# A sparse attention layer on one core: the first sort moved into the stream of its lists, feed-forward endings cut into steps, a sixth gather buffer and an earlier verdict

## The chip, the core and the metric

The kernel runs on one core of a Trainium2 chip. The core's engines work side by side, each through its own queue in order: TensorE (PE in the profile, PEld for its weight loads), VectorE (DVE), ScalarE (ACT), GpSimd (POOL) and SyncE (SP). SP, ACT and POOL also issue DMA transfers. The metric is the device time of one execution in microseconds (us), smaller is better.

## The reference, cut to what matters

One graph attention layer with a feed-forward block: N = 4096 nodes, D = 512, 8 heads of 64, float32. `adj` has a one for about 0.4% of the pairs and on the diagonal.

```
hs, ht = layer_norm(x), layer_norm(h_target)
q, k, v = ht @ Wq / 8, hs @ Wk, hs @ Wv            # per head
probs   = softmax(where(adj != 0, q k^T, -1e30))
ht      = layer_norm(ht + (probs @ v) @ Wo)
ff      = gelu(ht @ W1) @ W2                       # W1 512 x 2048, W2 2048 x 512
out     = layernorm(x + ht + ff)
```

## The kernel before

Since a row of `adj` has some 17 neighbours, the kernel never forms the 4096 x 4096 logits. It makes **lists** of neighbours, sorts the target nodes by degree, and then, tile by tile of 128 sorted targets, gathers one row of K and V (1024 floats) for each neighbour slot.

**Projections** (`project`). 16 groups of 256 source rows give K and V (`source`, L769), written to `kvd` in HBM (L773). 16 groups of target rows give q and a residual (`target`, L780), written to `tqd` (L791). Each group is normalised (`norm`: L628 on DVE, the power L622 on POOL, L623 on DVE, L741 on ACT), transposed (`turn`, L755) and multiplied. The targets form two parts: part 0 has 20 tiles (10 groups), part 1 has 12 tiles (6 groups, `qb`).

**Lists** (`edges`). For each of 32 tiles, four loads of `adj` on SP's queue (L637), a Sign on ACT (L640), and on DVE products and maxima (L642, L644), then 5 rounds of maximum and replace (L659, L661) that leave up to 40 neighbours in the record `R`.

**Sort** (`sort(part)`). A counting sort by degree: a one-hot `oh` (L687), four small matmuls (L697, L704) with scans between, ranks (L710), and one indirect store per tile on POOL (L713, 20 of them in part 0) that scatters the records to HBM. Its PSUM tile `t` is the one that `turn` uses too.

**Attention** (`attention`). Per tile, `prefetch` loads the sorted record (L824, SP), `front` gathers the targets' rows (`tq`, L812), and the neighbours are taken in stages of up to 3 slots. For a stage `issue` gathers 3 tiles of K and V (L812 on POOL, one instruction for each slot, into a `kv` buffer of 3 x 1024 floats); DVE multiplies by q (L944) and reduces (L948); ACT takes the exponential (L952); one stage later `values` multiplies V (L921), and PE sums by transposing into `cps` (L925), which frees the buffer. There are 5 `kv` buffers and `AHEAD = 3`. `finish` ends a tile: the softmax's sum, `Wo` (L882), `h` (L885), the norm (L621 to L623, L893) and its transposes (L901).

**Feed-forward** (`feed`). 17 groups of one or two tiles. `hidden` is W1 (L989) and gelu (L992), `output` is W2 (L998). The sums `po` begin with the transposes L1015, written after the second `hidden`. When a group ends, DVE adds (L1026), takes statistics, POOL the power (L622), DVE scales (L1030), and POOL stores the rows (L1032). `x` for the group is gathered half way (`xt`, L812).

**The order.** `_weave` merges generators by a clock of estimated costs, which each `yield` advances; nothing of it exists at run time. A compiler's scheduler takes the written order as priority, and may put a ready instruction further ahead in its engine's queue. Three weaves follow each other: (1) the projections of all sources and of part 0, beside the lists of part 0; (2) the rest of the projections, beside `begin` (sort of part 0, first records and gathers), from 55 the first 26 half stages of the attention, and from 60 two more tiles of lists; (3) the attention, the feed-forward, and the remaining 10 lists with the second sort. The weights `w1`, `w2` are loaded in quarters: the first between weaves 1 and 2 (when the sources' pool `src` is closed), three between 2 and 3 (when `mid` is closed). At the very end a verdict (did all sums, degrees and counts fit?) goes to `flag`, and `general_path` would run if it said no; with these inputs it does not run.

Of the kernel before, what the change touches and what calls it, by code (L numbers as in the profile page):

```python
# [17 lines left out]
P = 128  # L18
# [357 lines left out]
MAXE = 40  # L376
# [54 lines left out]
def adj_resnorm_kernel(  # L431
# [47 lines left out]
    SEGS = [(s * WQ // SQ, (s + 1) * WQ // SQ) for s in range(SQ)]  # L479
# [35 lines left out]
    with tc.tile_pool(name="keep", bufs=1) as keep:  # L515
# [14 lines left out]
        with ExitStack() as late:  # L530
            lp = late.enter_context(tc.tile_pool(name="lists", bufs=1))
            kp = late.enter_context(tc.tile_pool(name="kv", bufs=5))
# [19 lines left out]
            R = lp.tile([P, NT, RW], I32, name="R")  # L552
# [3 lines left out]
            iota_i = lp.tile([P, P], I32, name="iota_i")  # L556

            segoff = lp.tile([P, 2, NQ, SQ], F32, name="segoff")
            for b in range(2):
                for s, (w0, _) in enumerate(SEGS):  # L560
                    nc.gpsimd.iota(iota_i[:, :NQ], pattern=[[QW, NQ]], base=2 * w0 + b,
                                   channel_multiplier=0)
                    nc.vector.tensor_copy(segoff[:, b, :, s], iota_i[:, :NQ])

            nc.gpsimd.iota(iota_i, pattern=[[2, P]], base=1, channel_multiplier=0)
            lio = lp.tile([P, WQ], U16, name="lio")
            for w0, w1 in SEGS:
                nc.vector.tensor_copy(lio[:, w0:w1], iota_i[:, :w1 - w0])
            nc.gpsimd.iota(iota_i, pattern=[[1, P]], base=0, channel_multiplier=0)
            bins = lp.tile([P, NB], BF16, name="bins")  # L570
            nc.vector.tensor_copy(bins, iota_i[:, :NB])

            lower = lp.tile([P, P], BF16, name="lower")
            nc.gpsimd.memset(lower, -1.0)
            nc.gpsimd.affine_select(out=lower, in_=lower, compare_op=ALU.is_ge, fill=0.0, base=0,
                                    pattern=[[-1, P]], channel_multiplier=1)
            nc.gpsimd.memset(R, 0)
            nc.gpsimd.iota(R[:, :, MAXE + 1], pattern=[[P, NT]], base=0, channel_multiplier=1)
            for i0, n in PARTS:
                nc.gpsimd.iota(R[:, i0:i0 + n, MAXE + 2], pattern=[[P, n]], base=0,  # L580
                               channel_multiplier=1)
            one_c = lp.tile([P, 1], F32, name="one_c")
            nc.vector.memset(one_c, 1.0)
# [32 lines left out]
            def rstd_of(pool, mv, n, name):  # L616

                ve = pool.tile([P, n], F32, name=name + "_ve")
                rs = pool.tile([P, n], F32, name=name + "_rs")
                nm = pool.tile([P, n], F32, name=name + "_nm")  # L620
                nc.vector.tensor_scalar_add(ve, mv[:, :, 1], EPS)  # L621
                nc.gpsimd.tensor_tensor(rs, ve, mhalf[:, :n], ALU.pow)  # L622
                nc.vector.scalar_tensor_tensor(nm, mv[:, :, 0], -1.0, rs, op0=ALU.mult, op1=ALU.mult)  # L623
                return rs, nm
# [7 lines left out]
            def edges(i):  # L632

                cand = lp.tile([P, SEG, 8], U16, name="cand", bufs=2)
# [22 lines left out]
                for r in range(MAXE // 8):  # L657
                    top = R[:, i, r * 8:(r + 1) * 8]
# [4 lines left out]
                nc.vector.tensor_scalar(has, R[:, i, :MAXE], 0.0, 0.0, op0=ALU.is_gt,  # L663
# [7 lines left out]
            def sort(part):  # L671
# [3 lines left out]
                pool = lp  # L675
                nc.vector.tensor_reduce(deg[:, me], dpart[:, me, :], AX.X, ALU.add)
                nc.vector.tensor_copy(R[:, me, MAXE], deg[:, me])
# [7 lines left out]
                oh = pool.tile([P, NB * NA], BF16, name="oh")  # L685
# [26 lines left out]
                for i in range(n):  # L712
                    ins = nc.gpsimd.indirect_dma_start(  # L713
                        out=recs_d[part][:, :],
                        out_offset=bass.IndirectOffsetOnAxis(ap=ranki[:, i:i + 1], axis=0),
                        in_=R[:, i0 + i, :], in_offset=None)
# [135 lines left out]
            def finish(i, p, cps, group, hs, mv):  # L852
# [56 lines left out]
            def attention():  # L909
# [59 lines left out]
                while tails:  # L969
                    advance()  # L970
                    yield 3.0


            def feed(g):
# [49 lines left out]
                mv = sp.tile([P, 2, 2], F32, name="mv3")  # L1024
                for j in range(nt):
                    nc.vector.tensor_add(xs[j], po[j], xs[j])  # L1026
                    stats(sp, xs[j], mv[:, j, :], "n3")
                rs, _ = rstd_of(sp, mv[:, :nt, :], nt, "n3")
                for j, i in enumerate(group):
                    nc.vector.tensor_scalar(xs[j], xs[j], mv[:, j, 0:1], rs[:, j:j + 1],  # L1030
                                            op0=ALU.subtract, op1=ALU.mult)
                    ins = nc.gpsimd.indirect_dma_start(  # L1032
                        out=out[:, :], out_offset=bass.IndirectOffsetOnAxis(
                            ap=recs[i][:, MAXE + 1:MAXE + 2], axis=0),
                        in_=xs[j], in_offset=None)

                    tc.declare_no_dep(ins.ins, group="out", reason="other rows")
                    tc.add_to_no_dep_group("out", ins.ins)
# [6 lines left out]
            AHEAD = 3  # L1045
# [19 lines left out]
            wp1 = late.enter_context(tc.tile_pool(name="s2wa", bufs=1))  # L1065
            w1 = [wp1.tile([P, KC, D], F32, name="w1_0")]
            w2 = [wp1.tile([P, KC, D], F32, name="w2_0")]

            def load_quarter(q):
# [3 lines left out]
            load_quarter(0)  # L1073
            att = attention()
            early = 2 * sum(1 for i, _, _ in SG if i < 3)

            def begin():
# [10 lines left out]
            for q in range(1, 4):  # L1088
                w1.append(wp2.tile([P, KC, D], F32, name=f"w1_{q}"))
                w2.append(wp2.tile([P, KC, D], F32, name=f"w2_{q}"))  # L1090
                load_quarter(q)
# [8 lines left out]


        with tc.tile_pool(name="s3", bufs=1) as sp, \
                tc.tile_pool(name="s3ps", bufs=1, space=PSUM) as ps:
            sf = sums.rearrange("p t h -> p (t h)")
            ok = sp.tile([P, NT * H], F32, name="ok")
            nc.vector.tensor_scalar(ok, sf, SUM_LO, None, op0=ALU.is_gt)
            nc.vector.scalar_tensor_tensor(ok, sf, SUM_HI, ok, op0=ALU.is_lt, op1=ALU.mult)
            nc.vector.tensor_reduce(bad[:, 3:4], ok, AX.X, ALU.min)
            nc.vector.tensor_scalar(bad[:, 3:4], bad[:, 3:4], 1.0, None, op0=ALU.not_equal)
            over = sp.tile([P, NT], F32, name="over")  # L1110
            for i in range(NT):
                nc.vector.tensor_scalar(over[:, i:i + 1], degs[:, i:i + 1], float(TILES[i][1]), None,
                                        op0=ALU.is_gt)
            nc.vector.tensor_reduce(bad[:, 4:5], over, AX.X, ALU.max)
            nc.vector.tensor_scalar(over, degs, 1.0, None, op0=ALU.is_lt)
            nc.vector.tensor_reduce(bad[:, 5:6], over, AX.X, ALU.max)
            b1 = sp.tile([P, 1], BF16, name="b1")
            nc.vector.tensor_reduce(b1, bad, AX.X, ALU.max)
            pb = ps.tile([1, 1], F32, name="pb")
            nc.tensor.matmul(pb, b1, ones_bf[:, 0:1], start=True, stop=True)  # L1120
            nc.vector.tensor_scalar(flag, pb, 0.5, None, op0=ALU.is_gt)
# [35 lines left out]
```

## Time and profile before

| | us |
|---|---|
| median of 3 runs | 2008.25 (2004.03 to 2009.7) |
| the profiled execution | 2004.54 |
| its span, first to last instruction | 2002.8 |

| | busy us | share of the span |
|---|---|---|
| PE | 1751.0 | 87% |
| DVE | 1599.0 | 80% |
| POOL | 959.0 | 48% |
| ACT | 774.0 | 39% |

The profile's page gives busy shares, the same in 40 slices of the span, DMA queues, the chain of waits that ended last, and the costliest groups of instructions by line. The trace behind it answers for any stretch of time: busy time by engine with the clock that TensorE was granted, waits by who waited for whom, and the timeline. The lines that matter are shown in the prediction.

### The profile page before, as it was taken

The numbers are of one execution on the slowest core, as the hardware profiler recorded it, in microseconds if no ns is written. First come the engines' busy times: TensorE is split into PE (matmuls) and PEld (weight loads), VectorE is DVE, ScalarE is ACT, GpSimd is POOL, SyncE is SP. The second block draws the span as 40 slices with busy tenths as digits, with TensorE's granted clock in tenths as the row PEclk, the third lists the DMA queues.
The fourth block names the chain that finished last, engine by engine and source line by source line (L and its number), as shares of the span: only waits on it lengthen the run. The fifth ranks groups of instructions, "written<-read, shape, count | busy, mean of one in ns | idle before, by whom it ended". The sixth has DMA issues, their size and how long they took to land. (4 is left out here: it accounts for less than half of the span.)

```text
span 2002.8 us, 21520 instructions
## 1 busy us (share of the span) xinstructions
PE 1751.0 (87%) x7282; PEld 1133.6 (57%) x7282; DVE 1599.0 (80%) x2865; ACT 774.0 (39%) x1236; POOL 959.0 (48%) x879
## 2 busy tenths in 40 slices
PE   6989899762789999999798998989988889899996
PEld 3444444331556666666566666666665656567664
DVE  5989893356989999999788898988988878778601
ACT  5666564221245454452232333333323233333310
POOL 1023333164544546555666657657656554456301
PEclk9999999985979999998899999999999999999998
DMA  8778774479678888785578778868877766577300
GB/s 287 261 272 269 266 263 148 171 274 360 218 267 283 278 287 279 262 296 195 188 265 288 252 273 269 273 228 283 276 273 254 269 231 220 202 252 247 132 1 23
DMA packets 145391, 482.33 MB, mean 241 GB/s; under 512 B 20292, under 2 KB 20856, under 8 KB 145272
## 3 DMA queue, kind: packets, MB, share of 16 engines
q0 software_dynamic: 100032, 359.45, 52.2%
q1 hardware_dynamic: 39536, 102.53, 15.6%
q10 hardware_dynamic: 5704, 18.89, 2.4%
q8 instruction: 60, 0.98, 0.2%
q14 instruction: 59, 0.48, 0.1%
HBM read 438.07 MB, written 42.73 MB: 240 GB/s over the span
## 5 line engine op out<-in xcount | busy, mean ns | idle before, releaser
L812 POOL DMA_INDIRECT kv<-kvd,rec x600 | 687.6, 1146 | 464.6 <-PE cps L925 250.1
L989 PE MATMUL pf<-h2T,w 128*128 128x256 f32 (+1 forms) x2176 | 485.9, 374 | 3.6 <-ACT h2T L905 3.6
L998 PE MATMUL po<-w,gt 128*128 128x512 f32 x1024 | 471.1, 597 | 3.2 <-ACT gt L992 3.2
L944 DVE TENSOR_TENSOR kv<-kv,tq 128x1536 f32<-128x1536 f32 (+2 forms) x210 | 351.2, 1674 | 130.5 <-DMA kv<-kvd,rec 118.1
L989 PEld LDWEIGHTS pf<-h2T,w 128*128 128x128 f32 x2176 | 394.0, 195 | 77.2 <-issue 28.3
L925 PE MATMUL cps<-ident,kv 128*128 128x128 f32 x2400 | 320.4, 285 | 94.6 <-DVE kv L921 88.7
L925 PEld LDWEIGHTS cps<-ident,kv 128*128 128x128 f32 x2400 | 286.4, 147 | 169.3 <-DVE kv L921 127.3
L921 DVE TENSOR_TENSOR kv<-kv,p 128x1536 f32<-128x1536 f32 (+2 forms) x210 | 349.3, 1666 | 33.2 <-ACT p L952 33.0
L948 DVE TENSOR_REDUCE lg<-kv 128x24 f32<-128x1536 f32 (+2 forms) x210 | 349.3, 1666 | 0.5
L998 PEld LDWEIGHTS po<-w,gt 128*128 128x128 f32 x1024 | 186.5, 192 | 177.6 <-issue 171.6
L640 ACT ACTIVATE sg<-a 128x1024 uint8<-128x1024 int32 x128 | 135.0, 1055 | 146.5 <-DMA a<-in_adj_dram 90.4
L622 POOL TENSOR_TENSOR n_rs<-n_ve,mhalf 128x2 f32<-128x2 f32 (+1 forms) x66 | 55.0, 833 | 262.2 <-DVE n_ve L621 230.1
L952 ACT ACT_TABLE_LOAD x86 | 110.3, 1283 | 169.4 <-DVE lg L948 139.8
L952 ACT ACTIVATE p<-lg 128x24 f32<-128x24 f32 (+2 forms) x178 | 34.3, 193 | 320.3 <-DVE lg L948 161.4
L992 ACT ACTIVATE gt<-pf 128x512 f32<-128x512 f32 x128 | 76.5, 598 | 210.7 <-PE pf L989 190.2
L992 ACT ACT_TABLE_LOAD x111 | 142.4, 1283 | 2.0
L882 PE MATMUL t<-wo,rb 128*128 128x512 f32 x256 | 122.4, 623 | 20.3 <-DVE rb L878 20.3
L780 PE MATMUL pq<-wq,hT 128*128 128x512 f32 x256 | 125.2, 635 | 14.1 <-ACT row L771 7.5
L644 DVE MAX8 cand<-wd 128x8 uint16<-128x102 uint16 (+1 forms) x640 | 130.8, 251 | 0.8
L769 PE MATMUL pq<-wv,hT 128*128 128x512 f32 x256 | 116.1, 596 | 7.6 <-DVE row L783 6.8
L769 PE MATMUL pq<-wk,hT 128*128 128x512 f32 x256 | 116.0, 596 | 6.0 <-ACT row L771 3.7
L780 PEld LDWEIGHTS pq<-wq,hT 128*128 128x128 f32 x256 | 51.0, 206 | 78.8 <-issue 60.1
(122 smaller groups left out, 1452.0 us busy)
## 6 DMA issues: line engine op xcount, KB each, us to landing
a<-in_adj_dram SPq DMA_DIRECT2D x128, 512.0 KB
kvd<-row ACTq DMA_DIRECT2D x32, 512.0 KB
tq<-row POOLq DMA_DIRECT2D x20, 512.0 KB
kv<-kvd,rec POOLq DMA_INDIRECT x600
xin<-in_L_gnn_h_target_dram SPq DMA_DIRECT2D x16, 512.0 KB
w<-in_L_gnn_W_dram SPq DMA_DIRECT2D x8, 1024.0 KB
xin<-in_x_dram SPq DMA_DIRECT2D x15, 512.0 KB
tq<-row SPq DMA_DIRECT2D x12, 512.0 KB
```

What stands on the lines that cost most here:

```text
L640: nc.scalar.activation(sg, a, AF.Sign, accum_out=dpart[:, i, h:h + 1])
L769: nc.tensor.matmul(pkv, hT[:, kc, j * P:(j + 1) * P], w[:, kc, :], start=kc == 0, stop=kc == KC - 1)
L780: nc.tensor.matmul(pq, hT[:, kc, j * P:(j + 1) * P], wq[:, kc, :], start=kc == 0, stop=kc == KC - 1)
L812: nc.gpsimd.indirect_dma_start(out=dst, out_offset=None, in_=table[:, :], in_offset=bass.IndirectOffsetOnAxis(ap=idx, axis=0))
L921: nc.vector.tensor_tensor(v4, v4, p[:, j0:j0 + n, :].unsqueeze(3) .to_broadcast([P, n, H, HD]), ALU.mult)
L925: nc.tensor.matmul(cps[:, c, :], kv[:, j, D + c * P:D + (c + 1) * P], ident, is_transpose=True, start=j0 + j == 0 and c == 0, stop=j0 + j ...
L944: nc.vector.tensor_tensor(kv[:, :n, :D], kv[:, :n, :D], tq[:, :D].unsqueeze(1).to_broadcast([P, n, D]), ALU.mult)
L948: nc.vector.tensor_reduce(lg[:, :n, :], kv[:, :n, :D].rearrange("p j (h d) -> p j h d", h=H), AX.X, ALU.add)
L952: nc.scalar.activation(p[:, j0:j0 + n, :], lg[:, :n, :], AF.Exp)
L989: nc.tensor.matmul(pf[:, k, :], w1[(f0 + k) // KC][:, kc, (f0 + k) % KC * P:((f0 + k) % KC + 1) * P], h2T[:, kc, :w], start=kc == 0, stop= ...
L992: nc.scalar.activation(gt, pf, AF.Gelu_apprx_tanh)
L998: nc.tensor.matmul(po[j], gt[:, k, j * P:(j + 1) * P], w2[(f0 + k) // KC][:, (f0 + k) % KC, :], start=False, stop=f0 + k == FC - 1, skip_g ...
```

## The change

- **Part 0's sort** and first records join the stream of its lists in the first weave (`prepare`); `begin` then starts the attention 12 units after the records are there, in the same weave. `fill` makes three tiles of part 1's lists as soon as part 0's are done; 9 are left for the last weave. The four streams now run in one weave up to the closing of `mid`.
- **Constants** of the lists are written after the first projection's norm, with fewer and larger instructions. `R` and `oh` of part 0 move to the projections' pool, which gives room for
- **six `kv` buffers** instead of five, with `AHEAD = 4`.
- **Feed-forward ends** become a generator of four steps (`end`), one of which is taken after each of the next group's first four `hidden` (`wind_up`); `finish` too gets its power in a step of its own.
- **The verdict** is written at the end of the attention instead of the end of the kernel.

```diff
-    SEGS = [(s * WQ // SQ, (s + 1) * WQ // SQ) for s in range(SQ)]
+    WS = -(-WQ // SQ)
+    SEGS = [(s * WS, min(s * WS + WS, WQ)) for s in range(SQ)]
...
-            kp = late.enter_context(tc.tile_pool(name="kv", bufs=5))
+            kp = late.enter_context(tc.tile_pool(name="kv", bufs=6))
...
-            R = lp.tile([P, NT, RW], I32, name="R")
+            Rs = [pool.tile([P, n, RW], I32, name=f"R{i}")
+                  for i, (pool, (_, n)) in enumerate(zip((wp, lp), PARTS))]
...
+            def list_constants():
+                io = lp.tile([P, QW], I32, name="a", bufs=2)
+                nc.gpsimd.iota(io[:, :SQ * WS], pattern=[[0, SQ], [2, WS]], base=1,
+                               channel_multiplier=0)
...
-                oh = pool.tile([P, NB * NA], BF16, name="oh")
+                if part:
+                    oh = sp.tile([P, MAXE, H], F32, name="pm", bufs=1)
+                    oh = oh.rearrange("p j h -> p (j h)").bitcast(BF16)
+                else:
+                    oh = wp.tile([P, NB * n], BF16, name="oh")
...
-                rs, nm = rstd_of(sp, mv[:, :len(hs), :], len(hs), "n2")
+                nh = len(hs)
+                ve = shifted(sp, mv[:, :nh, :], nh, "n2")
                 yield
+                rs = power(sp, mv[:, :nh, :], nh, "n2", ve)
+                yield
+                nm = negmean(sp, mv[:, :nh, :], rs, nh, "n2")
...
                 while tails:
                     advance()
                     yield 3.0
-
+                verdict()
...
+            def end(group, xs, po):
+
+                nt = len(group)
+                mv = sp.tile([P, 2, 2], F32, name="mv3")
+                for j in range(nt):
+                    nc.vector.tensor_add(xs[j], po[j], xs[j])
+                    stats(sp, xs[j], mv[:, j, :], "n3")
+                ve = shifted(sp, mv[:, :nt, :], nt, "n3")
+                yield
+                rs = power(sp, mv[:, :nt, :], nt, "n3", ve)
+                yield
+                for j in range(nt):
+                    nc.vector.tensor_scalar(xs[j], xs[j], mv[:, j, 0:1], rs[:, j:j + 1],
+                                            op0=ALU.subtract, op1=ALU.mult)
+                yield
+                for j, i in enumerate(group):
+                    ins = nc.gpsimd.indirect_dma_start(
...
+                def wind_up():
+                    for e in list(ends):
+                        if next(e, StopIteration) is StopIteration:
+                            ends.remove(e)
+
                 last = hidden(0)
+                wind_up()
                 yield cost
                 for f0 in range(fb, FC, fb):
                     now = hidden(f0)
+                    wind_up()
                     yield cost
...
-            AHEAD = 3
+            AHEAD = 4
...
-            _weave((_take(proj, both * G), 0), (_take(ed, NA * steps), 0))
-            src.close()
...
             next(proj)
+            list_constants()
...
+            def projections():
+                yield from _take(proj, both * G)
+                src.close()
+                load_quarter(late.enter_context(tc.tile_pool(name="s2wa", bufs=1)), 0)
+                yield from proj
+
+            def prepare():
+
+                yield from _take(ed, NA * steps)
+                ready.append("lists")
                 yield from sort(0)
+                while not w1:
+                    yield None
                 for i in range(2):
                     prefetch(i)
                 next(att)
+                ready.append("rows")
+
+            def fill():
+
+                while not ready:
+                    yield None
+                for cost in _take(ed, 3 * steps):
+                    yield 2.0 * cost
+
+            def begin():
+                while len(ready) < 2:
+                    yield None
+                yield 12.0
+                yield from _take(att, early)
...
-            _weave((proj, 0), (begin(), 0), (_take(att, early), 55), (_take(ed, 2 * steps), 60))
+            _weave((projections(), 0), (prepare(), 0), (fill(), 0), (begin(), 0))
             mid.close()
```

More of the change, by code (lines that the diff above doesn't have):

```diff
@@ L632, in edges @@
             def edges(i):
+                part = 1 if i >= NA else 0
+                rec = Rs[part][:, i - PARTS[part][0], :]
                 cand = lp.tile([P, SEG, 8], U16, name="cand", bufs=2)
@@ L662, in edges @@
                 has = lp.tile([P, MAXE], F32, name="ehas")
[L663 removed]
+                nc.vector.tensor_scalar(has, rec[:, :MAXE], 0.0, 0.0, op0=ALU.is_gt,
                                         op1=ALU.add, accum_out=cnt[:, i:i + 1])
@@ L971, in attention, with verdict @@
                     yield 3.0
+                verdict()
+            def verdict():
+                sf = sums.rearrange("p t h -> p (t h)")
+                both = sp.tile([P, MAXE, H], F32, name="pm", bufs=1).rearrange("p j h -> p (j h)")
+                ok, over = both[:, :NT * H], both[:, NT * H:NT * H + NT]
+                nc.vector.tensor_scalar(ok, sf, SUM_LO, None, op0=ALU.is_gt)
+                nc.vector.scalar_tensor_tensor(ok, sf, SUM_HI, ok, op0=ALU.is_lt, op1=ALU.mult)
+                nc.vector.tensor_reduce(bad[:, 3:4], ok, AX.X, ALU.min)
+                nc.vector.tensor_scalar(bad[:, 3:4], bad[:, 3:4], 1.0, None, op0=ALU.not_equal)
+                for i in range(NT):
+                    nc.vector.tensor_scalar(over[:, i:i + 1], degs[:, i:i + 1], float(TILES[i][1]),
+                                            None, op0=ALU.is_gt)
+                nc.vector.tensor_reduce(bad[:, 4:5], over, AX.X, ALU.max)
+                nc.vector.tensor_scalar(over, degs, 1.0, None, op0=ALU.is_lt)
+                nc.vector.tensor_reduce(bad[:, 5:6], over, AX.X, ALU.max)
+                b1 = sp.tile([P, 1], BF16, name="b1", bufs=1)
+                nc.vector.tensor_reduce(b1, bad, AX.X, ALU.max)
+                pb = ps.tile([1, 1], F32, name="t")
+                nc.tensor.matmul(pb, b1, ones_bf[:, 0:1], start=True, stop=True)
+                nc.vector.tensor_scalar(flag, pb, 0.5, None, op0=ALU.is_gt)
@@ new lines, in adj_resnorm_kernel @@
+            ends = []
+            def end(group, xs, po):
[14 more added lines that the diff above has]
+                    ins = nc.gpsimd.indirect_dma_start(
+                        out=out[:, :], out_offset=bass.IndirectOffsetOnAxis(
+                            ap=recs[i][:, MAXE + 1:MAXE + 2], axis=0),
+                        in_=xs[j], in_offset=None)
+                    tc.declare_no_dep(ins.ins, group="out", reason="other rows")
+                    tc.add_to_no_dep_group("out", ins.ins)
@@ L1023, in feed @@
                 yield cost
[L1024 to L1038, printed above, removed]
+                ends.append(end(group, xs, po))
+                if g + 1 == len(GROUPS):
+                    for _ in ends.pop():
+                        pass
             def chain(gens):
@@ L1081, in begin @@
                 next(att)
-            _weave((proj, 0), (begin(), 0), (_take(att, early), 55), (_take(ed, 2 * steps), 60))
+                ready.append("rows")
[9 more added lines that the diff above has]
+                yield from _take(att, early)
+            ready = []
+            att = attention()
+            early = 2 * sum(1 for i, _, _ in SG if i < 3)
+            _weave((projections(), 0), (prepare(), 0), (fill(), 0), (begin(), 0))
             mid.close()
@@ L1099, in adj_resnorm_kernel @@
                    (other_lists(), t0))
[L1102 to L1121, printed above, removed]
     left = nc.values_load(flag[0:1, 0:1], min_val=0, max_val=1)
```

76 lines of the change are left out of this document (38 added, 38 removed).

## The prediction, made before the result was known

> **What bounds the kernel now.** I began with the page's 40 slices, 50 us each (digits are tenths busy; PEclk is the clock that TensorE was granted).
>
> ```profile
> span 2002.8 us, 21520 instructions
> PE   6989899762789999999798998989988889899996
> DVE  5989893356989999999788898988988878778601
> PEclk9999999985979999998899999999999999999998
> ```
>
> Three regimes show. Up to slice 6 PE is nearly full (projections). In slices 7 to 11 both PE and DVE fall, the clock with them. From slice 12 (600 us) PE stands at 8 or 9, DVE beside it. So there is no single bound: where PE is full, only PE's work counts; where both have holes, something else ends last. Hence the busy table by stretch: from:to, length, then PE, PEld, DVE, ACT and POOL with instructions, PE's clock, DMA share, GB/s.
>
> ```profile
> 310.00:367.00 57.00, 56.48 (x162) 26.95 (x160) 13.86 (x37) 22.53 (x41) 14.01 (x15) 1.00 0.37 129
> 367.00:390.00 23.00, 18.19 (x54) 8.76 (x53) 12.35 (x16) 5.48 (x11) 0.00 (x0) 0.93 0.67 228
> 390.00:422.00 32.00, 20.32 (x50) 10.09 (x49) 16.18 (x54) 11.60 (x20) 22.93 (x24) 0.79 0.47 162
> 422.00:437.00 15.00, 11.00 (x32) 5.01 (x30) 7.37 (x24) 5.19 (x10) 10.41 (x11) 0.97 0.98 349
> 437.00:482.00 45.00, 15.72 (x52) 10.92 (x52) 41.65 (x74) 3.33 (x10) 25.45 (x20) 0.58 1.00 381
> 482.00:503.00 21.00, 1.12 (x4) 0.71 (x4) 1.28 (x3) 3.49 (x7) 1.29 (x1) 0.50 0.91 341
> 503.00:523.00 20.00, 12.03 (x61) 8.64 (x62) 20.00 (x24) 2.09 (x6) 10.82 (x10) 0.88 0.63 204
> 523.00:600.00 77.00, 65.64 (x340) 47.96 (x340) 68.15 (x125) 33.55 (x54) 38.66 (x34) 0.87 0.74 250
> ...
> 600.00:900.00 300.00, 295.67 (x1323) 202.90 (x1322) 297.05 (x569) 145.01 (x217) 164.47 (x143) 1.00 0.81 280
> 900.00:1000.00 100.00, 85.15 (x359) 60.19 (x358) 83.91 (x116) 28.46 (x43) 59.73 (x53) 0.86 0.58 193
> 1000.00:1900.00 900.00, 813.16 (x3767) 569.57 (x3766) 761.74 (x758) 312.96 (x454) 528.97 (x466) 0.97 0.73 249
> 1900.00:1988.00 88.00, 83.19 (x355) 55.21 (x353) 9.32 (x23) 9.36 (x17) 6.70 (x8) 0.99 0.05 16
> ```
>
> From 367 to 600, PE is busy 144 of 233 us, and what it does at a lower clock costs some 23 more (each row's busy time times one minus its clock). Some 112 us of PE's time are lost there. From 600 to 900, PE and DVE are both full: nothing to win but by less work. From 1000 to 1900, PE lacks 87 us and DVE 138. After 1900 PE is full to the end.
>
> **First term: the start of the attention.** The timeline (start, duration, engine, idle time before and what ended it):
>
> ```profile
> 309.97 1.16 DVE L687 TENSOR_TENSOR oh<-b,bins 128x960 bf16<-128x960 bf16 x1
> ...
> 368.01 0.33 ACTq L773 DMA_DIRECT2D kvd<-row  x1
> ...
> 372.37 0.37 PE L697 MATMUL t<-oh,ones_bf 128*128 128x480 bf16 x1
> ...
> 378.40 0.56 PE L697 MATMUL t<-oh,ones_bf 128*128 128x480 bf16 x1 [4.81 <-DVE a L698]
> ...
> 390.42 1.31 POOL L713 DMA_INDIRECT rec<-R,ranki  x1 [38.20 <-DVE ranki L710]
> ...
> 417.07 0.96 POOL L713 DMA_INDIRECT rec<-R,ranki  x1 [0.30 <-issue]
> ...
> 421.80 1.03 POOL L812 DMA_INDIRECT tq<-tq,rec  x1 [2.05 <-DMA rec<-rec]
> ...
> 437.17 1.76 DVE L944 TENSOR_TENSOR kv<-kv,tq 128x1536 f32<-128x1536 f32 x1 [4.84 <-DMA kv<-kvd,rec]
> ```
>
> The sort's one-hot is ready at 311, but its first matmul stands in PE's queue behind all projections of the first weave and runs at 372. Then come the ranks, 20 scatters (390 to 418), and only at 421.8 the first gather.
>
> In the weave's units, lists of part 0 cost 20 x 14 = 280, sort and scatters 20 + 20 x 1.3 = 46, the projections of that weave 32 x 7.8 + 20 x 4.3 = 335.6. The last store of K and V was issued at 368, so a unit is 1.10 us (280 units are 307 us; the row says 310). In the changed order the scatters are written at 326 units, 358 us, ahead of the last projections. Their time lies beside PE: from 310 to 367 DVE has 43 us to spare and POOL 43, where the 20 scatters took 28. Also `fill` writes two of its three tiles there (280 + 56 = 336 units). The cover costs a little: the sort's matmuls share PSUM tile `t` with `turn`, and PE stood 4.81 us between the two L697. I let the projections end 5 us later, at 373. Gathers need the last K and V store landed; from the last scatter to the first gather it took 3.8 us with a record load besides, so I put the gather at 376 instead of 422: **46 us**.
>
> Does it pass on? DVE idles 100 us between 310 and 523 and PE loses 112 until 600, so there is room. What could come late next: the powers L622 of the last six target groups, which queue on POOL behind the first 15 gathers, now five stages deep, and behind them PE's transposes; in the old order they queued behind the scatters and PE waited just as well. And this:
>
> ```profile
> 497.72 1.06 ACT L640 ACTIVATE sg<-a 128x1024 uint8<-128x1024 int32 x1 [22.55 <-DMA a<-in_adj_dram]
> ```
>
> ACT stands 22.6 us for an `adj` load that queues behind three quarters of the weights, and every exponential stands behind it. The change writes the weights ahead of the next lists as before, so I count on that hole again. Bounds: 15 us, if this stretch is held by transfers alone (0.9 to 1.0 busy from 422 to 503); 65, if the hole goes too. The Trainium skill (DMA: Bandwidth & Descriptors, Specifications) limits HBM to some 358 GB/s for a core; by it, the 33.6 MB moved from 422 to 523 would need 94 us instead of 88 at the 381 GB/s of the row. The row is above the page, and the measurement decides.
>
> **Second term: six buffers.** Waits between 1000 and 1900 (who for whom: us in total, times, longest):
>
> ```profile
> POOL kv L812 <- PE cps L925: 129.9, 61, 10.3
> DVE kv L944 <- DMA kv<-kvd,rec: 96.8, 44, 5.9
> POOL tq L812 <- DVE h L885: 48.8, 9, 8.3
> PE cps L925 <- DVE kv L921: 40.1, 22, 5.9
> PE t L882 <- DVE rb L878: 20.1, 8, 5.5
> ```
>
> A circle: POOL waits for a buffer that PE has summed, DVE for the gather, PE for DVE. One turn of it:
>
> ```profile
> 1350.14 0.94 POOL L812 DMA_INDIRECT kv<-kvd,rec  x1 [10.25 <-PE cps L925]
> ...
> 1358.41 1.76 DVE L944 TENSOR_TENSOR kv<-kv,tq 128x1536 f32<-128x1536 f32 x1 [5.23 <-DMA kv<-kvd,rec]
> ```
>
> A free buffer is data 8.3 us later. One more buffer is one more stage that has landed, 3 x 1.75 = 5.2 us of DVE work (L944, L948 and L921 have that length). The 44 waits are 2.2 us on average and 5.9 at most; a burst shares its cover, so I let three quarters go, some 73 us of DVE. PE then binds: 813 busy, of its 87 idle the 40 behind L921 fall to some 10, the rest stays, and less idling gives back half of the 24 us that a clock of 0.97 costs. 813 + 57 - 12 = 858, say 855 for 900: **45 us**. Bounds: nothing, and 111 (PE never idle at full clock, 789).
>
> From 900 to 1000 PE idles 15 us and loses 12 to its clock, while the second sort's scatters hold POOL's queue. A stage more in hand covers part: **6 us** (0 to 27). From 600 to 900 nothing: PE is full. One list less there takes work off DVE alone.
>
> **Third term: the rest.** The endings keep their instructions, in other places. The verdict leaves this tail:
>
> ```profile
> 1983.74 0.13 DVE L1121 TENSOR_SCALAR flag<-pb 1x1 int32<-1x1 f32 x1
> ```
>
> With the slot around it some **1 us**. The constants: nothing (0 to 5; slice 0 has 16 us of PE idle, but loads of weights set its end).
>
> Sum: 46 + 45 + 6 + 1 = 98 from the profiled execution's 2004.5: 1906.5. The median of the runs stands 0.2% above it (2008.25), which makes 1910; I say 1908.
>
> **Rivals.**
>
> *The buffer brings nothing; POOL binds* (1953, the second term lost). For it: POOL already stands 49 us on `tq` gathers, which wait for `h` of three tiles before with kv gathers queued behind, and `tq` keeps three buffers. Against it: POOL is busy 59% of that stage. The gathers by stretch, 600 to 900 and then 1000 to 1900 (count, busy, mean ns, idle before), and their least, median and longest:
>
> ```profile
> L812 POOL DMA_INDIRECT kv<-kvd,rec x118 | 137.7, 1167 | 101.5 <-PE cps L925 54.0 <-issue 27.2 <-DVE lg L948 7.7
> ...
> L812 POOL DMA_INDIRECT kv<-kvd,rec x389 | 443.7, 1141 | 242.4 <-PE cps L925 129.9 <-issue 91.5 <-remote 4.5
> ...
> L812 POOL DMA_INDIRECT kv<-kvd,rec x600: 932/943/2532, 423.1 to 1865.0; - x150
> ```
>
> A denser DVE hardly lengthens a gather: 1167 ns where DVE is 99% busy, 1141 where it is 85%. By the Trainium skill (SBUF — State Buffer, "SBUF: two separate sides") a DVE operation with two SBUF inputs and a GpSimd operation that reads SBUF exclude each other for the whole instruction; were every gather held like the longest, 389 x 2.53 us would overfill the stage. The 2532 ns bear the lock out, the means say that it is rare; its chance is part of this rival's.
>
> *The early start is eaten* (1944: of 46 us 10 remain). The sort is early, but weights, ACT's hole and the target groups fill the time, and the feed-forward begins hardly sooner. For it: DMA at 0.9 to 1.0 until 503. Against it: from 310 to 422 DMA is 0.37 to 0.67 busy, and the earlier gathers go there.
>
> *Slower: the endings hold PE* (2030). L1026 frees `po`, and L1015 of the next group waits for it.
>
> ```profile
> 1317.77 1.28 DVE L1026 TENSOR_TENSOR xt<-po,xt 128x512 f32<-128x512 f32 x2
> ...
> 1319.30 5.78 PE L989 MATMUL pf<-h2T,w 128*128 128x256 f32 x26
> 1324.91 1.04 PE L1015 MATMUL po<-ident,h2T 128*128 128x128 f32 x8
> ```
>
> Now L1026 ends 5.9 us before L1015. The change writes it behind the first `hidden`, so only the second (16 matmuls, some 3.5 us) lies between. Should DVE come to L1026 a stage and its own length late (5.2 + 1.3) plus a place in its queue, PE stands 7 to 8 us at each of 16 borders, 120 us, 22 more than the gain. It decides from 98 / 16 = 6.1 us a border. Against it: DVE gets ahead with six buffers.
>
> *It does not do what it says*: PE's queue still holds the sort back and the buffers stay unused: 1985 to 2000. *More than thought*: start 65, stage 80, the hundred 12: 1848.
>
> **How the numbers follow.** Forecast 0.50; buffer brings nothing 0.17; start eaten 0.15; more than thought 0.09; slower 0.06; no effect 0.03. The range 1860 to 1962 leaves out the last three, 0.18. About 0.3% (6 us) is what a measurement of this kernel can tell from no change. Faster by more: 0.92; within: 0.02; slower: 0.06.
>
> **What would show it.** First step: L713 ends before 365, the first `kv` gather stands near 376, the first W1 matmul (L989) of a two-tile group some 45 us earlier. Second: DVE's waits for `kv` gathers from 1000 on fall to a quarter, PE above 94% there. PE waits for DVE before L1015 would show the slower rival; a POOL above 70% with DVE still waiting, the first. Wrong altogether if the hole of 482 to 503 grows, or if the last six target groups end later than before.

## The result, and the profile after

The changed kernel takes **1910.4 us** (median of 4 runs, 1909.8 to 1911.3) where the kernel before took 2006.1 in the runs beside it (1999.5 to 2009.7). The ratio is 0.953, its 95% interval 0.950 to 0.955. The profiled execution took 1911.0, its span 1909.3. The forecast was 1908.

The page's slices of the changed kernel, 48 us each:

```profile
span 1909.3 us, 21425 instructions
...
PE   6999989767989999995999999999999989999995
...
DVE  5899997568999999997888899999999987788500
...
PEclk9999999898989999997999999999999999999998
```

The dip of slices 7 to 11 is down to slices 7 to 9, from 334 to 477 us, and none of them is under 6. A single 5 (slice 18, the second sort) stands behind it. From slice 19 on PE is at 9 nearly throughout.

To see in which stage the time was saved, each run is cut at the same events: the third, the tenth, the thirteenth and the last `h` (h2, h9, h12, h31: the DVE addition at L885 before and L907 after). The busy table by these stages, columns as in the prediction, first of the kernel before:

```profile
310.00:577.00 267.00, 183.43 (x674) 104.95 (x671) 158.05 (x299) 75.03 (x137) 108.51 (x100) 0.83 0.67 238
577.00:864.00 287.00, 277.11 (x1236) 192.13 (x1236) 283.84 (x555) 141.42 (x216) 159.29 (x140) 0.98 0.82 283
864.00:1010.00 146.00, 130.78 (x563) 91.67 (x561) 128.15 (x188) 46.34 (x68) 87.22 (x76) 0.91 0.66 224
1010.00:1913.00 903.00, 816.16 (x3774) 571.46 (x3774) 754.27 (x754) 312.57 (x454) 522.46 (x460) 0.97 0.72 246
```

And of the changed kernel:

```profile
310.00:537.00 227.00, 176.35 (x671) 100.51 (x670) 168.90 (x343) 79.81 (x146) 107.77 (x101) 0.90 0.80 294
537.00:822.00 285.00, 275.34 (x1243) 191.38 (x1241) 282.94 (x550) 143.07 (x213) 164.58 (x141) 0.98 0.81 282
822.00:970.00 148.00, 122.61 (x546) 85.03 (x545) 129.11 (x150) 40.54 (x62) 86.11 (x77) 0.92 0.64 222
970.00:1819.00 849.00, 808.93 (x3791) 568.55 (x3790) 742.49 (x737) 308.95 (x450) 523.82 (x456) 0.98 0.76 258
```

Forty us come from the start, two from the stage in which both engines are full, none from the second sort (148 for 146), and 54 from h12 to h31. In that last stage PE's idle time fell from 87 us to 40. The waits there in the changed kernel (who for whom: us in total, times, longest):

```profile
POOL kv L834 <- PE cps L951: 89.3, 49, 8.5
...
DVE kv L970 <- DMA kv<-kvd,rec: 65.7, 38, 7.0
POOL n_rs L634 <- DVE n_ve L627: 49.4, 15, 15.3
POOL tq L834 <- DVE h L907: 43.2, 7, 11.5
...
PE t L904 <- DVE rb L900: 24.2, 9, 5.6
PE cps L951 <- DVE kv L947: 3.8, 5, 1.9
```

Of the two waits on which the second term rested, PE's for the weighted values went from 40.1 us to 3.8, but DVE's for gathers only from some 95 to 65.7, not to a quarter. DVE still waits; it no longer holds PE. The start did not go as drawn either. Its timeline in the changed kernel:

```profile
356.26 0.63 POOL L813 DMA_DIRECT2D tq<-row  x1
...
358.35 1.01 POOL L735 DMA_INDIRECT rec<-R,ranki  x1 [0.17 <-issue]
...
362.04 1.07 ACT L793 COPY row<-pq 128x512 f32<-128x512 f32 x2 [13.76 <-DMA tq<-row]
...
362.68 5.72 PE L791 MATMUL pq<-wk,hT 128*128 128x512 f32 x8 [13.00 <-ACT row L793]
...
384.42 3.60 PE L791 MATMUL pq<-wv,hT 128*128 128x512 f32 x8
...
390.48 0.39 SPq L1139 DMA_DIRECT2D w<-in_L_gnn_W_dram  x1
...
391.45 0.33 ACTq L795 DMA_DIRECT2D kvd<-row  x1
...
400.83 1.01 POOL L834 DMA_INDIRECT kv<-kvd,rec  x1 [22.22 <-DMA w<-in_L_gnn_W_dram]
```

The last scatter ends at 359, as forecast. But a store of target rows (L813), whose row was ready at 345, stood behind eight scatters in POOL's queue until 356, and it held a `row` buffer until it had landed. So ACT could not empty PSUM (where TensorE writes its sums) for 13.8 us, PE stood 13.0, and the projections ended at 388, not 373. The last store of K and V then went out at 391, a microsecond behind the first 2 MB of weights, and the first `kv` gather came at 401, 12.8 us after the last K and V matmul, for which the prediction had allowed 3. So the gather was 25 us later than forecast, 15 of them by the projections and 10 by what lies between them and the gather. Three things had to be tested: what the start is worth, what the buffer is worth, and whether the endings, priced at nothing, really are worth nothing.

### The profile page after: what moved, and what is told of

Its sections match the earlier page's. It is cut to its first block, busy times and chain, and to the rows that moved or that the text cites. A ratio compares the mean times of both kernels' runs of the same rounds, so it can differ in the third digit from the quotient of the medians.

```text
span 1909.3 us, 21425 instructions
## 1 busy us (share of the span) xinstructions
PE 1727.1 (90%) x7282; PEld 1118.6 (59%) x7282; DVE 1596.2 (84%) x2835; ACT 771.9 (40%) x1234; POOL 963.6 (50%) x872
## 2 busy tenths in 40 slices
DMA packets 145391, 482.33 MB, mean 253 GB/s; under 512 B 20292, under 2 KB 20856, under 8 KB 145272
## 3 DMA queue, kind: packets, MB, share of 16 engines
HBM read 438.07 MB, written 42.73 MB: 252 GB/s over the span
## 4 chain that ended last, share of the span: by engine, by line
DVE 38%; DMA 21%; PE 15%; issue 12%; POOL 10%; ACT 3%; SPq 0%; DVEq 0%; POOLq 0%; ACTq 0%
DMA kv<-kvd,rec 10%; DVE kv L970 9%; DVE kv L947 7%; POOL kv L834 7%; DVE lg L974 6%; PE pf L1063 5%; PE po L1072 4%; DMA a<-in_adj_dram 4%; DVE cand L662 3%; PE t L904 2%; DVE n_st L644 2%; PE cps L951 2%; DMA xin<-in_L_gnn_h_target_dram 2%; DVE R L677 2%; DVE gid L679 2%
## 5 line engine op out<-in xcount | busy, mean ns | idle before, releaser
L834 POOL DMA_INDIRECT kv<-kvd,rec x600 | 703.6, 1173 | 385.4 <-PE cps L951 175.1
L1063 PE MATMUL pf<-h2T,w 128*128 128x256 f32 (+1 forms) x2176 | 474.5, 369 | 2.3 <-ACT h2T L931 2.1
L1063 PEld LDWEIGHTS pf<-h2T,w 128*128 128x128 f32 x2176 | 387.2, 191 | 72.3 <-issue 24.6
L951 PE MATMUL cps<-ident,kv 128*128 128x128 f32 x2400 | 307.9, 277 | 34.1 <-DVE kv L947 33.7
L951 PEld LDWEIGHTS cps<-ident,kv 128*128 128x128 f32 x2400 | 278.3, 143 | 100.1 <-DVE kv L947 55.2
L904 PE MATMUL t<-wo,rb 128*128 128x512 f32 x256 | 130.1, 655 | 27.5 <-DVE rb L900 27.4
L791 PE MATMUL pq<-wk,hT 128*128 128x512 f32 x256 | 120.0, 612 | 20.9 <-ACT row L793 17.1
L662 DVE MAX8 cand<-wd 128x8 uint16<-128x103 uint16 (+1 forms) x640 | 132.9, 253 | 0.8
L802 PE MATMUL pq<-wq,hT 128*128 128x512 f32 x256 | 117.8, 604 | 9.0 <-DVE row L805 5.3
L904 PEld LDWEIGHTS t<-wo,rb 128*128 128x128 f32 x256 | 52.2, 211 | 89.0 <-issue 55.6
```

The costliest lines, as they stand in the source:

```text
L662: nc.vector.max(cand[:, h * SQ + s, :], wd[:, w0:w1])
L791: nc.tensor.matmul(pkv, hT[:, kc, j * P:(j + 1) * P], w[:, kc, :], start=kc == 0, stop=kc == KC - 1)
L834: nc.gpsimd.indirect_dma_start(out=dst, out_offset=None, in_=table[:, :], in_offset=bass.IndirectOffsetOnAxis(ap=idx, axis=0))
L904: nc.tensor.matmul(pa, ct[:, c, :], wo[:, c, :], start=c == 0, stop=c == KC - 1)
L951: nc.tensor.matmul(cps[:, c, :], kv[:, j, D + c * P:D + (c + 1) * P], ident, is_transpose=True, start=j0 + j == 0 and c == 0, stop=j0 + j ...
L1063: nc.tensor.matmul(pf[:, k, :], w1[(f0 + k) // KC][:, kc, (f0 + k) % KC * P:((f0 + k) % KC + 1) * P], h2T[:, kc, :w], start=kc == 0, stop= ...
```

## The experiments

All are edits of the changed kernel. Its 1910.4 is the mark for medians, its stages above for the rest. Kernels of the same start varied in their profiled runs: the first `h` fell at 482 in the changed kernel and between 485 and 488 in six runs whose edits lie behind it or hardly touch it. The third, h2, fell at 537 in the changed kernel and between 543 and 546 in the five of these that have six buffers. So what is read up to h2 is sure only to some 9 us.

**Five buffers again.**

```diff
-            kp = late.enter_context(tc.tile_pool(name="kv", bufs=6))
+            kp = late.enter_context(tc.tile_pool(name="kv", bufs=5))
...
-            AHEAD = 4
+            AHEAD = 3
```

> Five kv buffers and AHEAD 3 again, everything else as changed. Theory (the sixth buffer gave the 54 us of tiles 12 to 31): about 1960 us (1945 to 1972), PE's wait before the cps matmuls (L947 to L951) from the end of h12 on back from 4 to some 40 us, the stage h12 to h31 back from 849 to about 900, the start to h2 as changed (537). Rival (the endings in steps gave it, the buffer is unused): about 1915 (1908 to 1922) with PE's wait at cps still under 10 us. If both give: 1930 to 1945.

Measured: 1962.4 (1960.5 to 1966.8), 52 more. The first and last stage, and two waits of the last:

```profile
310.00:553.00 243.00, 188.13 (x695) 106.51 (x693) 179.04 (x382) 81.94 (x151) 109.34 (x103) 0.89 0.78 278
...
988.00:1871.00 883.00, 816.34 (x3783) 572.72 (x3782) 750.66 (x741) 312.16 (x453) 518.48 (x457) 0.98 0.74 249
```

```profile
DVE kv L970 <- DMA kv<-kvd,rec: 73.4, 41, 5.7
...
PE cps L951 <- DVE kv L947: 24.2, 12, 4.2
```

The total is as the theory said, the places are not quite. The buffer is worth 34 us in the last stage (883 for 849: 27 of PE's idle time, and 7 in which it is busy longer). Up to h2 the run is 16 us longer than the changed kernel, but only 7 to 10 longer than the other runs of the same start with six buffers. DVE's waits for gathers hardly changed with it (73 for 66); PE's did (24 for 4).

**Six buffers, gathers written one stage later** (`AHEAD = 3` alone).

> Six kv buffers, but AHEAD 3: gathers are written one stage later; all else as changed. The run with five buffers and AHEAD 3 took 1962. Theory (the buffer is what counts; the place in which gathers are written matters little, since POOL's queue already stood on full buffers): 1910 to 1918. Rival (a buffer is of no use unless the gather is written early enough): 1940 to 1962.

Measured: 1911.9 (1910.5 to 1915.9). The place in which gathers are written counts for nothing; the buffer does. From the run before, this one differs in the buffer alone: 50 us in all, 31 of them in the last stage (851 for 883).

**Endings at once again.**

```diff
+                rs = power(sp, mv[:, :nh, :], nh, "n2", ve)
+                nm = negmean(sp, mv[:, :nh, :], rs, nh, "n2")
                 yield
-                rs = power(sp, mv[:, :nh, :], nh, "n2", ve)
-                yield
-                nm = negmean(sp, mv[:, :nh, :], rs, nh, "n2")
...
-                ends.append(end(group, xs, po))
-                if g + 1 == len(GROUPS):
-                    for _ in ends.pop():
-                        pass
+                for _ in end(group, xs, po):
+                    pass
```

> The feed-forward's ending runs at once again, behind the last W2 matmul, and finish takes its power in the step of the sums; six buffers, start and verdict as changed. Theory (the buffer gave the late gain, the endings almost nothing): 1910 to 1918 us. Rival (the endings in steps are what freed PE): 1940 to 1960, with PE's waits for DVE at the transposes and the scores doubled. The other side (the endings hold PE in front of the next po group, as the slower rival of the prediction said): under 1905.

Measured: 1936.6 (1930.7 to 1939.9), 26 more. The endings count, against the prediction.

**Of these, only the edit in `finish`** (the first hunk; endings in steps).

> Of the two edits undone together before (1937 us, 26 more than the change) only the one in finish is undone: its power of the row sums is written in the step of the sums again; the feed-forward's ending stays in steps. Theory A (the ending in steps is worth the 26): 1910 to 1917. Theory B (finish's power is: POOL waited for n_ve with kv gathers queued behind): 1930 to 1938. Both halves: 1920 to 1928.

Measured: 1915.8 (1915.5 to 1917.6). Its 5 us over the change are there at the first `h` already (488 for 482), ahead of the edited code, so nothing is shown for the power's own step in `finish`. The 21 us between the two runs are the feed-forward's ending in steps. The last stage with endings in steps, then at once:

```profile
980.00:1826.00 846.00, 803.89 (x3781) 564.93 (x3780) 741.76 (x737) 308.69 (x450) 518.04 (x455) 0.99 0.76 259
```

```profile
985.00:1845.00 860.00, 810.23 (x3789) 569.77 (x3788) 742.78 (x738) 306.20 (x448) 523.55 (x456) 0.98 0.75 255
```

Of the 21, 14 lie in the last stage, half of them idle time of PE, half longer work of PE (clock 0.98 for 0.99); no single wait of PE stands out (the largest, for `rb`, went from 26.4 to 30.0). POOL's waits for sums of squares and for `h` grew from 102 to 115. That these, with gathers queued behind them, are the path is possible, not shown.

**The old order of the start** (the two old weaves in place of the four streams).

```diff
-            _weave((projections(), 0), (prepare(), 0), (fill(), 0), (begin(), 0))
+            _weave((_take(proj, both * G), 0), (_take(ed, NA * steps), 0))
...
+            _weave((proj, 0), (old_begin(), 0), (_take(att, early), 55), (_take(ed, 2 * steps), 60))
```

> The old two-part order of the start (target lists and projections first, then sort, first rows and source lists beside the rest of the projections), everything else as changed. Theory (the start is worth the 41 us that h2 came earlier): 1951 us (1943 to 1958), h2 back from 537 to about 577, the stage from h12 on unchanged at about 849. Rival (the earlier start is partly taken back behind h2, because the same DMA work has to fit somewhere): 1925 to 1940.

Measured: 1935.6 (1930.2 to 1937.8), 25 more, in the rival's range. Its stages:

```profile
310.00:574.00 264.00, 186.59 (x675) 107.69 (x674) 158.23 (x298) 75.38 (x139) 108.00 (x101) 0.82 0.68 246
574.00:860.00 286.00, 276.68 (x1245) 191.92 (x1243) 284.62 (x557) 140.44 (x213) 157.46 (x139) 0.98 0.82 285
860.00:1002.00 142.00, 131.21 (x576) 90.08 (x575) 128.76 (x187) 42.95 (x66) 92.51 (x79) 0.94 0.67 229
1002.00:1845.00 843.00, 798.91 (x3759) 562.50 (x3758) 750.32 (x745) 304.07 (x447) 537.10 (x457) 0.99 0.77 262
```

It comes to h2 37 us late and makes 12 of them good from h9 on (142 for 148, 843 for 849). The early start is worth 25 us at the end, not 37. Against the other runs of the same start h2 is only 28 to 31 us late, so less than 12 may have been made good. That the same transfers take it back, as the rival says, is not shown.

**Stores of the target rows on SP's queue.**

```diff
-                    eng, dma = (nc.vector, nc.sync) if part else (nc.gpsimd, nc.gpsimd)
+                    eng, dma = (nc.vector, nc.sync) if part else (nc.gpsimd, nc.sync)
```

> One word: the stores of the target rows go out on SP's queue in place of POOL's, so that none stands behind the 20 scatters. Theory (the row tiles held by such a store stopped ACT, and with it PE for 13 us at 362, and moved the last projection from 367 to 388): that hole of PE goes to under 3 us, the last K/V matmul ends before 378, the first kv gather stands near 385 to 390 instead of 401, h2 ends 10 to 16 us earlier, and the time is about 1897 us (1893 to 1902). Rival (PE's hole isn't on the path, the weights and gathers until 437 set the end of the start anyway, or SP's queue takes it back): 1907 to 1914, with the hole gone and h2 within 4 us of 537.

Measured: 1911.6 (1901.3 to 1918.3), the last K/V matmul at 384, the first `kv` gather at 402.9: no gain. PE's longest hole there was 6.7 us, half of what it was, but the projections had come to it 5 us later, and the scatters ran from 342 to 370 instead of 329 to 359. So neither the theory nor the rival, by which the hole goes, describes it. **Source lists later** (`fill` begins when `ready` has two entries), alone and with that edit:

> The three source lists of fill begin when the first rows are requested (ready has two entries), not beside the sort. Theory (their Sign operations on ACT, which wait for adj loads, and their DMA hold the last projections back): the last K/V matmul ends before 380 instead of 391, the first kv gather stands before 392 instead of 401, h2 ends 8 to 15 us earlier, 1897 to 1904. Rival (POOL's 20 scatters hold them, by the stores and powers queued behind): projections and first gather within 4 us of the change, and the lists then missing cost time later: 1912 to 1930.

> Both: fill begins with the first rows, and the target rows' stores go out on SP's queue. Theory (two causes, each of which hides the other: taken alone the stores changed nothing): projections end before 374, the first kv gather before 385, 1890 to 1900. Rival (transfers hold the stretch from 400 to 440 whatever comes before): first gather earlier by 10 us or more, but h2 within 5 us of 537, 1908 to 1918.

Measured: 1919.7 (1916.2 to 1923.4) and 1920.0 (1911.5 to 1928.1), some 9 more each. In the first PE's hole is 15.4 us, the projections end at 404 and the first gather stands at 414; only the time lies in the rival's range. In the second the hole is 13.2 us and the gather at 405, and the time misses both ranges. The lists did not hold the projections here. What did is seen in the second run, from which the stores are gone:

```profile
353.08 0.15 DVE L627 TENSOR_SCALAR n_ve<-mv 128x2 f32<-128x2 f32 x1
...
367.88 0.74 POOL L634 TENSOR_TENSOR n_rs<-n_ve,mhalf 128x2 f32<-128x2 f32 x1
368.65 0.16 DVE L639 SCALAR_TENSOR_TENSOR n_nm<-mv,n_rs 128x2 f32<-128x2 f32 x1 [14.90 <-POOL n_rs L634]
...
368.84 1.52 ACT L763 ACTIVATE xin<-xin,n_nm,n_rs 128x512 f32<-128x512 f32 x2 [18.21 <-DVE n_nm L639]
...
370.88 4.47 PE L791 MATMUL pq<-wv,hT 128*128 128x512 f32 x5 [13.17 <-ACT row L793]
```

The sums are ready at 353, their power runs on POOL at 368, when the last scatter is through; DVE, ACT and PE wait in a row. With the store gone from POOL's queue, the power of the next norm is what stands behind the scatters.

**POOL's queue cleared.** The last norms take their power on DVE (`newton`: a first value from the float's bits, three steps of Newton's iteration; eleven small instructions on 128x2), and the last two target groups of the part use DVE and SP.

```diff
-                    rs, nm = rstd_of(ip, mv, G, "n1")
+                    rs, nm = (newton if n >= 22 else rstd_of)(ip, mv, G, "n1")
...
-                    eng, dma = (nc.vector, nc.sync) if part else (nc.gpsimd, nc.gpsimd)
+                    eng, dma = (nc.vector, nc.sync) if g >= 8 else (nc.gpsimd, nc.gpsimd)
```

> POOL's queue is cleared beside the 20 scatters of the first sort: the last norms of the projections (from the 23rd group on) take their power in steps on DVE instead of on POOL, and the last two target groups' row operations and stores go to DVE and SP. Theory (whatever the projections have in POOL's queue stands behind 25 us of scatters; the stores alone only moved the wait to the powers): PE's hole of 13 us goes, the last K/V matmul ends before 376 instead of 388, the first kv gather stands before 390 instead of 401 to 408, and if transfers then leave room, 1895 to 1903. Rival (the stretch to 440 is held by transfers): gather early, h2 within 5 us of 537 to 546, 1906 to 1914. Other side (DVE, 14 to 18 of 20 us busy there, becomes the bound of the start): over 1916.

Measured: **1900.6** (1900.0 to 1902.0), ratio 0.948 (0.946 to 0.950), the shortest of all:

```profile
355.56 0.96 POOL L750 DMA_INDIRECT rec<-R,ranki  x1 [0.30 <-issue]
...
394.58 0.94 POOL L849 DMA_INDIRECT kv<-kvd,rec  x1 [28.32 <-DMA kvd<-row]
```

```profile
364.05 1.06 ACT L673 ACTIVATE sg<-a 128x1024 uint8<-128x1024 int32 x1 [6.01 <-DMA a<-in_adj_dram]
```

```profile
369.17 6.17 PE L806 MATMUL pq<-wv,hT 128*128 128x512 f32 x8 [7.73 <-ACT row L808]
...
379.49 3.69 PE L806 MATMUL pq<-wv,hT 128*128 128x512 f32 x8
```

The hole shrinks from 13.0 to 7.7 us, the projections end 5 us earlier and the gather comes 6 earlier (13 against runs whose start was the later one). The time is in the theory's range, but its signs (no hole, last matmul before 376, gather before 390) are not reached. This fits POOL's queue as one cause. Half of the hole stays: ACT then waits 6.0 us for an `adj` load of the later lists at 364, with DMA 0.91 busy from 360 to 380. Whether later lists would help now was not run. At h2 the run is 2 us ahead of the changed kernel, at h9 7; where the rest comes from is not shown.

**What DVE still waits for.** From the second sort on, query rows of every other tile go into list buffers that are free by then:

```diff
-                tq = sp.tile([P, 2 * D], F32, name="tq", bufs=3)
+                if 1 in done and i % 2:
+                    tq = lp.tile([P, QW], I32, name="a", bufs=2).bitcast(F32)
+                else:
+                    tq = sp.tile([P, 2 * D], F32, name="tq", bufs=3)
```

> From the second sort on, every other tile takes its query rows in the list buffers that are free by then, so that a tq gather no longer waits for h of three tiles before (POOL stood 43 us so from h12 to h31, kv gathers behind it). Theory (of DVE's 66 us for kv gathers left there, part comes from gathers queued behind that wait, which is why a sixth buffer took only a third of the 95): POOL's wait for h under 8, DVE's wait for kv gathers under 50, 1890 to 1902. Rival (POOL then stands the same time on full kv buffers, PE binds): 1907 to 1913.

Measured: 1914.4 (1911.7 to 1924.4). POOL's wait for `h` fell from 43.2 us to some 6, DVE's for gathers from 65.7 to 60.6, the last stage took 846 for 849. That is what the rival says, its time a microsecond above the range. POOL stood on full buffers instead (116.8 for 89.3).

**Powers a step later** (one more `yield` behind each `shifted`). With it the ending of the last group but one lacks its last step: two tiles' rows are not stored.

> One more step between the sum of squares and its power, in finish and in the feed-forward's ending, so that POOL comes to the power later (it stood 49 to 64 us on n_ve, kv gathers behind it). Theory (POOL's head-of-line waits hold gathers back): POOL's wait for n_ve halves, DVE's wait for kv gathers under 55, 1895 to 1905. Rival (POOL only stands elsewhere): 1907 to 1914. Other side (h of the group ends a step later, and h2T and the feed-forward's ends with it): 1916 to 1930.

Measured: 1904.1 (1900.9 to 1907.2); DVE's wait for gathers 48.4, the last stage 840. The time and DVE's wait are as the theory says, but POOL's wait for the sums of squares did not halve (41.1 for 49.4).

> The two edits that gained, together, the second carried through: powers and rows of the last projections off POOL (1900.6 alone, 9.8 less than the change), and the power of finish and of the feed-forward's ending one step later, with every ending still open run out behind the last group (that run without it, and without the store of two tiles' rows, was 1904, 6 less). Theory (they lie in different stages and add up): 1891 to 1897, stage h12 to h31 840 to 843 as in the run with later powers, projections ended by 384. Rival (the later powers owed their gain to the two stores left out): 1898 to 1902, with that stage at 846 to 849.

Measured: 1908.0, but between 1901.7 and 1924.6 in six runs. The profiled one took 1924.6, the longest; its last stage was 845 with DVE's wait at 47.8, and its first gather came at 406, not 395. Neither theory holds: the sum didn't come, and later powers aren't told apart from nothing. In that execution the time was lost before h2 (549 for 535 with POOL cleared alone), and PE had its hole although nothing but scatters stood in POOL's queue from 335 to 360:

```profile
363.24 0.69 DVE L820 SCALAR_TENSOR_TENSOR row<-pq,bq 128x512 f32<-128x512 f32 x1 [11.92 <-remote]
...
363.98 6.42 PE L806 MATMUL pq<-wv,hT 128*128 128x512 f32 x8 [12.30 <-DVE row L820]
```

DVE and ACT both wait until 363 for something that the profile does not name ("remote"), while transfers nearly stand (16 GB/s from 356 to 362). So the shorter hole of the run above is one profile against another, and clearing POOL's queue doesn't always bring it. What holds DVE here, and why these six times spread over 23 us where the four of the run above lie within 2, stays open.

## Why the prediction was right, step by step

- **The total** (1906.5 worked out, 1908 said, 1910.4 measured) was right. That it came so near is luck: the start brought some 20 us less than was counted, the endings some 20 that were not counted.
- **Start, 46 us:** 40 by the stage to h2, of which the sixth buffer has a share; 25 by the run with the old order. Two steps failed. "I let the projections end 5 us later" priced the sort's matmuls on PE, not what its 20 scatters do on POOL, where powers, row operations and stores of the same projections queue: 21 us, not 5. Some 15 of the 21 are PE's hole behind the store and the slower matmuls after it (5.7 us for eight, 3.6 elsewhere). I had looked for powers behind gathers, and behind scatters in the old order only. The other step is the 3 us between the projections' end and the first gather: they follow a wait for a record load, and with the last store of K and V it was 12.8. So the sign "first gather near 376" failed (401, where the first `kv` gather before stood at 423). The first W1 matmul of a two-tile group came 41 us earlier (546.1 for 587.2), near the 45 forecast. ACT's hole, counted on again, came in two parts, 10.7 and 9.1 us for `adj` loads in place of 22.6. The hole of PE that was not to grow (1.1 us busy of the 21 from 482) is now 4.8 of the 21 from 412.
- **Buffer, 45 us:** 50 to 52 by the two runs that show it, 31 to 34 of them in the stage for which it was worked out and most of the rest before h9, where none was counted. PE's side was right: idle behind the values 10 forecast, 3.8 measured, PE at 95%. That the stage from h12 to h31 took 849 us where 855 were forecast from 1000 to 1900 is luck in part: 14 of the 54 us gained there are the endings. DVE's side was wrong: a quarter of its waits was to remain, two thirds did, and the sixth buffer took only 8 us of them (73.4 to 65.7). Why the rest stays is open; it cost little, since PE hardly waits behind it.
- **Endings, nothing:** 21. They were weighed as a risk at `po` alone. That wait never came: PE does not wait once before L1096 in the whole run. That they also gain was not asked, and how they gain is open.
- **Second sort, 6 us:** nothing came (148 for 146). **Verdict, 1 us:** nothing either; from h31 to the end of the span both kernels take 90 us.
- **The rivals:** POOL as the bound falls: it is 62% busy from h12 on, and its wait for `h` taken away gains nothing. The early start was eaten in part, at most 12 of 37 us. The last target groups did end later (last L802 at 464.7 us, the same matmul before, L780, at 444.3), which the prediction gave as a sign of its failure; it wasn't one, as those groups are wanted only much later.

The parts taken back one by one give 25 + 52 + 26 = 103 us for the 96 gained together. As each of them carries the 5 us or so by which the start varies, this doesn't show whether they relieve partly the same waits.

## What to carry to other kernels

When a block of instructions moves beside other work, price it on every queue that it enters, and list what the neighbours have in that queue: here 25 us of scatters on POOL stood ahead of a store in one run and of a power in another, and each time PE had a hole of 13 us. An engine's waits are worth only what the bound engine waits behind them: DVE kept two thirds of its waits, and PE waited 4 us for DVE's values instead of 40. And a part that looks like mere reordering needs a price on both sides, not as a risk alone. A total that fits does not show that its parts do.

## What the runs showed of the hardware

Transfers ran faster than the 381 GB/s of the kernel before. The busy table of the changed kernel from 420 to 440 us

```profile
420.00:440.00 20.00, 7.09 (x25) 5.27 (x26) 12.95 (x20) 7.42 (x14) 6.16 (x7) 0.66 1.03 413
```

shows 413 GB/s, all 16 engines busy. Nearly all of what is moved goes to or from HBM: over the run 438.07 MB read and 42.73 MB written of 482.33 MB. The limit of some 358 GB/s that the prediction cites is thus not one for this core in these runs. The Trainium skill (DMA: Bandwidth & Descriptors, "Where 436 GB/s comes from") gives 435 as what the 16 ports can carry; the row lies 5% under that.
